# A two-layer graph attention kernel: where layer 2's one-hot matrices lie, when they are loaded, and when layer 2's gathers may begin

## The chip, the cores and the metric

The kernel runs on one core of a Trainium2 chip. Its time is the device time of one execution in microseconds. Beside the times there is one profiled execution, taken by the hardware profiler; its trace lists every instruction with its start, its length and what ended the wait before it. The engines are TensorE (PE; its weight loads are listed as PEld), VectorE (DVE), ScalarE (ACT), GpSimd (POOL) and SyncE (SP). SP, ACT and POOL also issue DMA transfers, which all run on the core's 16 DMA engines.

## The reference

A layer norm and a relu are applied to 3125 nodes of 768 features. Then come two graph attention layers over 53,125 edges (each edge in both directions, and a loop for every node), sorted by their target node:

```
xl = (x @ W).reshape(n, heads, out_ch)
e = leaky_relu(alpha_src[src] + alpha_dst[dst], 0.2)
alpha = softmax of e over the edges of one target
out = segment_sum(xl[src] * alpha, dst) + bias
```

Layer 1 has 4 heads of 256 columns, followed by a layer norm, a relu and a residual product `h0 @ Wr1 + br1`. Layer 2 has one head of 768 columns, followed by a layer norm and `h1 @ Wr2 + br2`. The input is added at the end.

## The kernel before

The nodes are cut into 25 blocks of 128 targets (the last has 53). Every block owns J = 17 lists of 128 edge slots, its tiles; the last block uses 8 of them. The work of a layer has three parts.

**The products.** `x @ W` gives a table in HBM, one row for each node, and two numbers for each node, alpha_src and alpha_dst. In layer 1's sums the function `end1` (L1217) finishes a block: it normalizes, turns the block with PE, multiplies by W2 (L1260), and stores a block of `h1T_d` and a block of `table2` through SP's queue. Layer 2 can gather when all of table2 is stored.

**The weights of the edges.** For each edge the kernel needs alpha_src of its source and alpha_dst of its target. Both are picked by products with one-hot matrices. These were made in layer 1 and kept in HBM, in fp8, as `hot_d`: for each block 128 rows of 2176 + 640 + 425 bytes. In layer 2 a loop over the 25 blocks (L1355) multiplies them: 51 matmuls of 25 columns (`source_values`, L552) and 5 of 24 columns (`own_products`, L535) for each block. DVE then masks and sums the results (L554, L541, L557). I call this the one-hot loop. The matrices lie in a ring of 4 buffers (`load_hot`, L1288). The first four blocks are loaded through POOL's queue (L1292), the others through SP's, each when the loop has come to it and a buffer is free (L1357). After the loop, `shares` (L644) turns the sums into weights, with two scans on DVE.

**The sums.** `sums` (L704) goes over the blocks and in each over five rounds of tiles. `fetch` (L769) gathers 128 rows of the table for each tile with one indirect DMA on POOL (L779), and PE adds them, weighted, into the block's rows (L826). In layer 1 the gathers go to 13 buffers of 4096 bytes, g0 to g12 in turn; there are 416 of them. In layer 2 they go to a ring of 26 buffers of 771 words (`ahead` is 26), also 416 of them. Between the rounds PE does other work that the code hands out in steps. In layer 2 that is the residual product `h1 @ Wr2` (L1326, and L1330 for the bias), 18 matmuls for each block, one block ahead. The residual of block 0 is done near the end of the one-hot loop (`fill`, L1367).

**The order.** PE's order is written out by hand in the one-hot loop, and PE's, ACT's and DVE's in the sums. Everything else is ordered by a planner that goes by its own estimates; every queue runs its instructions in order. Two rules bear on the change. `behind` is a copy of one number on POOL (L1370, into `mark`), which waits for the sums of one block of the one-hot loop; all gathers of layer 2 stand behind it on POOL's queue. `last_hot` is the last load of a one-hot matrix; what SP loads for the sums stands behind it on SP's queue.

Layer 2's tiles lie in the memory that layer 1 leaves, and a tile waits only for those that lay in its own place. The layer-2 constants, wr2, the four one-hot buffers and three buffers of h1 end at one point; the 26 gather buffers begin there, each taking 3104 bytes.

Of the kernel before, what the change touches and what calls it, by code (L numbers as in the profile page):

```python
# [10 lines left out]
F32 = mybir.dt.float32  # L11
F32R = mybir.dt.float32r
BF16 = mybir.dt.bfloat16
F8 = mybir.dt.float8e4
# [9 lines left out]
PE = mybir.EngineType.PE  # L24
# [16 lines left out]
HOT = 3264  # L41
# [28 lines left out]
def in_order(  # L70
# [16 lines left out]
    nc = tc.nc  # L87
# [6 lines left out]
    NB = -(-N // P)  # L94
# [22 lines left out]
    def rows_of(b):  # L117
        return P if b < NB - 1 else LAST
# [4 lines left out]
    def tiles_of(b):  # L123
        return J if b < NB - 1 else JL
# [64 lines left out]
    def load_rows(q, t, src_, b):  # L189

        for o, e in pieces(b):
            q.dma_start(t[o:e], src_[b * P + o:b * P + e, :])
# [306 lines left out]
    def parts_of(pool, v, n, name):  # L499

        part = pool.tile([P, 3, n], BF16, name=name, bufs=1)
        rest = pool.tile([P, n], F32, name=name + "_r", bufs=1)
        nc.vector.tensor_copy(part[:, 0, :], v)  # L503
        nc.vector.tensor_sub(rest, v, part[:, 0, :])
        nc.vector.tensor_copy(part[:, 1, :], rest)
        nc.vector.tensor_sub(part[:, 2, :], rest, part[:, 1, :])
        return part
# [15 lines left out]
    def by_quarter(t, v, n, heads):  # L523

        for i in range(3):
            nc.vector.tensor_tensor(t[:, :, :, i, :], v(i)[:, :, None, :].to_broadcast([P, n, 4, 2 * heads]),
                                    mine[:, None, :, None].to_broadcast([P, n, 4, 2 * heads]), OP.mult)

    def own_products(heads, pp, oh, tabd_b, bufs=1):

        n = 6 * heads
        pd = pp.tile([128, 512], F32, name="pd", bufs=bufs)[:, :J * n]
        for c in range(WIN // 128):
            o = FROM[c % 4] + c // 4
            nc.tensor.matmul(pd[:, o * n:(o + 4) * n], oh[:, c * 128:(c + 1) * 128],  # L535
                             tabd_b.rearrange("p q t v -> p (q t v)"), start=(c == 0), stop=True,
                             skip_group_check=True)
        return pd.rearrange("p (j t v) -> p v j t", t=3, v=2 * heads)

    def own_values(own, b, pd):  # L540
        nc.vector.tensor_reduce(own[:, :, :, b].rearrange("p j v -> p v j"), pd, axis=AX.X, op=OP.add)  # L541
# [162 lines left out]
    def sums(heads, cols, table, al, alo_d, ahead, lag, gp, ap, pp, end, more, pace, first=None, delay=0.0):  # L704
# [4 lines left out]
        width = heads * cols  # L709
        f = width // 2  # L710
# [48 lines left out]
        def ask(b):  # L759
            ao = asked[b] = ap.tile([128, 2 * heads, NB], F32, name="ao", bufs=3)  # L760
            nc.gpsimd.indirect_dma_start(
                out=ao.rearrange("p v b -> p (v b)"), out_offset=None, in_=alo_d[:, :],
                in_offset=bass.IndirectOffsetOnAxis(ap=at_last[:, b:b + 1], axis=0))

        extra = 3 if heads == 1 else 0
        turns = count()
        owns = {}

        def fetch(b, k):  # L769

            got = {}
            for j in ROUNDS[k]:
                if j >= tiles_of(b):
                    continue
                if heads == 1:
                    g = gp.tile([128, width + extra], F32, name="g", bufs=ahead)
                else:
                    g = gp.tile([128, width], F32, name=f"g{next(turns) % ahead}", bufs=1)
                nc.gpsimd.indirect_dma_start(  # L779
                    out=g[:, :width], out_offset=None, in_=table[:, :],  # L780
                    in_offset=bass.IndirectOffsetOnAxis(ap=idx_s[:, b * J + j:b * J + j + 1], axis=0))
                if heads == 1:
                    nc.scalar.activation(g[:, width:], alo_d[:, POS[j], b, :], AF.Copy)
                got[j] = g, weights_of(b, j)
                place = PLACE[j]
                if place == 4:
                    own = owns[b] = ap.tile([128, width], F32, name="own", bufs=3)
                    load_rows(nc.sync, own, table, b)
                if heads > 1 and b == 1 and place == 11:
                    ask(0)  # L790
                if heads > 1 and b and place == (13 if tiles_of(b) == J else 5):
                    ask(b)
            return got

        def weights_of(b, j):

            c = b * J + j
            lo, hi = 32 * QUARTERS[j][0], 32 * QUARTERS[j][-1] + 32
            w = ap.tile([128, heads, hi - lo], F32, name=f"w{hi - lo}", bufs=9 if hi - lo == 32 else 3)
            if heads == 1:  # L800
                nc.vector.tensor_scalar(w[:, 0, :], iota_f[:, lo:hi], rel_s[:, c:c + 1], al[:, POS[j], 0, b:b + 1],  # L801
                                        op0=OP.is_equal, op1=OP.mult)
            else:
                oh = ap.tile([128, 68], F32, name="oh", bufs=4)[:, :hi - lo]
                nc.vector.tensor_scalar(oh, iota_f[:, lo:hi], rel_s[:, c:c + 1], None, op0=OP.is_equal)  # L805
                nc.vector.tensor_tensor(w, oh[:, None, :].to_broadcast([128, heads, hi - lo]),  # L806
                                        al[:, POS[j], :, b:b + 1].to_broadcast([128, heads, hi - lo]), OP.mult)
            return w
# [33 lines left out]
    with tc.tile_pool(name="m1", bufs=1) as mp:  # L842
# [8 lines left out]
        with tc.tile_pool(name="h0", bufs=1) as hp, tc.tile_pool(name="pm1", bufs=1, space=PSUM) as pm1, \  # L851
# [5 lines left out]
            so = right.enter_context(tc.tile_pool(name="so1", bufs=1, side="right"))  # L857
# [415 lines left out]
    with tc.tile_pool(name="m2", bufs=1, reuse_waits="tile") as mp, \  # L1273
# [12 lines left out]
        hots = {}  # L1286

        def load_hot(b, q):  # L1288
            hots[b] = mp.tile([128, HOT], F8, name="hot", bufs=4)
            return q.dma_start(hots[b][:, :S + WIN + J * NB], hot_d[b, :, :S + WIN + J * NB]).ins  # L1290

        for b in range(4):  # L1292
# [8 lines left out]
        def load_h1(b, q):  # L1301
            h1 = h1s[b] = mp.tile([128, NK2, P], F32, name="h1", bufs=3)
            r = rows_of(b)
            q.dma_start(h1[:, :, :r], h1T_d[b][:, :, :r])

        for b in range(2):
            load_h1(b, nc.gpsimd)
        loaded = {}

        def load(b):  # L1310
# [26 lines left out]
        def ahead_of(first, end, apart):  # L1337
            load(first)
            load(first + 1)
            for b in range(first, end):  # L1340
                load(b + 2)
                yield from residual(b, apart)

        with tc.tile_pool(name="ps2", bufs=1, space=PSUM, reuse_waits="tile") as pp:
            fill = ahead_of(0, FIRST, 5)
            with tc.tile_pool(name="so2", bufs=1, side="right", reuse_waits="tile") as so, \
                    tc.manual_schedule(engines={PE}):
                al = wide[:, :, None, :]
                with tc.tile_pool(name="sb2", bufs=2, side="right", reuse_waits="tile") as sb:
                    part = parts_of(sb, asad2.rearrange("p b v -> p (b v)"), NB * 2, "part")  # L1350
                    v = lambda i: part[:, i, :].rearrange("p (b v) -> p b v", v=2)
                    by_quarter(tabd, v, NB, 1)
                    for i in range(3):
                        nc.vector.tensor_copy(tabs[:, i], v(i)[:, :, :1].rearrange("p b h -> p h b"))
                    for b in range(NB):  # L1355
                        if b not in hots:
                            last_hot = load_hot(b, nc.sync)  # L1357
                        hot = hots.pop(b)
                        pick = picks.pop() if picks else mp.tile([128, J, 1, NB], F32, name="pick", bufs=2)
                        source_values(1, al, b, pp, 3, J, hot, tabs,  # L1360
                                      hot[:, S + WIN:S + WIN + J * NB].rearrange("p (j b) -> p j b", b=NB), pick)
                        own_values(own, b, own_products(1, pp, hot[:, S:S + WIN], tabd[:, b]))
                        if b == NB - 10:
                            with tc.issue_after(last_hot):
                                load(0)
                        if b > NB - 4:
                            with tc.issue_after(last_hot):  # L1367
                                next(fill)
                        if b == NB - 11:
                            behind = nc.gpsimd.tensor_copy(mark, al[:, 0, 0, b:b + 1]).ins  # L1370
                with tc.tile_pool(name="sr2", bufs=1, side="right", reuse_waits="tile") as sr:
                    shares(wide, own, al2[:, :, 0, :], ends2, sr, pp, fill, (5, 4))
                for _ in fill:
                    pass
# [493 lines left out]
```

## Time and profile before

| | |
|---|---|
| three runs | 1989.29 us (median), 1982.86 to 1989.85 |
| the profiled execution | 1990.46 us, of which 1988.6 are the span of the trace |
| PE busy | 1793.4 us, 90% |
| DVE busy | 1060.1 us, 53% |
| POOL busy | 902.0 us, 45% |
| HBM traffic | 290 GB/s over the span |
| last layer-1 gather issued | 1210.57 us |
| last store of table2 issued | 1268.28 us |
| first matmul of the one-hot loop | 1270.99 us |
| first matmul of layer 2's sums | 1368.75 us |

Busy time is an average over stages with different limits. A group's row gives the line, the engine, the operation, its tiles and its count, then busy time and the mean of one instruction in ns, then how long its engine sat idle just before it and what ended that. "issue" is time in which an engine waited for nothing that the profile shows. In a row of a timeline the first number is the start in us, the second the length, and the bracket the idle time before it with what ended it. A row of windows has a stretch and its length, then busy time and count for PE, PEld, DVE, ACT and POOL, then the granted TensorE clock, the mean busy share of the 16 DMA engines, and what they moved.

### The profile page before, as it was taken

What the parts mean: (1) busy time and instruction counts of PE and PEld (TensorE: products, weight loads), DVE (VectorE), ACT (ScalarE), POOL (GpSimd) and SP (SyncE); (2) the same over time, 40 slices, a digit from 0 to 9 for tenths busy, and PEclk for the clock granted to TensorE, in tenths of its full rate; (3) what the DMA queues carried; (4) which work ended last, traced back from release to release, by engine and by line L of the source; (5) the groups of instructions that cost most, each with busy time, mean ns of one, the idle gap of its engine ahead of it and who ended that gap; (6) DMA issues with size and microseconds to landing.
All of it is one profiled execution on the core that took longest, in us unless ns stands there. A gap on an engine that the chain in (4) does not pass through costs nothing. (4 is left out here: it accounts for less than half of the span.)

```text
span 1988.6 us, 34126 instructions
## 1 busy us (share of the span) xinstructions
PE 1793.4 (90%) x12558; PEld 985.9 (50%) x12558; DVE 1060.1 (53%) x3030; ACT 295.5 (15%) x1094; POOL 902.0 (45%) x977
## 2 busy tenths in 40 slices
PE   8999999998779999999998998838989888998986
PEld 5666665664446555565544554534333333333332
DVE  7673437886645555655566454524444444444445
ACT  2122331001211221221111211101000000000000
POOL 2000101112455566566656653052666666666662
PEclk9999999998889999999999999858999998999999
DMA  7823448774699999999999996486999999999984
GB/s 244 267 96 132 129 144 205 177 176 152 229 408 352 386 375 396 381 381 408 391 392 367 376 362 264 142 286 207 338 327 327 328 328 325 330 338 323 341 284 147
DMA packets 180786, 574.86 MB, mean 289 GB/s; under 512 B 32768, under 2 KB 55034, under 8 KB 180485
## 3 DMA queue, kind: packets, MB, share of 16 engines
q0 software_dynamic: 108432, 408.63, 57.5%
q1 hardware_dynamic: 67786, 153.57, 22.5%
q10 hardware_dynamic: 4394, 10.39, 1.3%
q8 instruction: 103, 1.69, 0.3%
q14 instruction: 71, 0.57, 0.1%
HBM read 503.27 MB, written 73.85 MB: 290 GB/s over the span
## 5 line engine op out<-in xcount | busy, mean ns | idle before, releaser
L779 POOL DMA_INDIRECT g<-table,idx_s x832 | 816.3, 981 | 555.6 <-issue 208.6
L826 PE MATMUL pa<-g,w 128*32 128x256 f32 (+2 forms) x5868 | 527.9, 429 | 69.5 <-issue 52.6
L826 PEld LDWEIGHTS pa<-g,w 128*32 128x32 f32 x5868 | 204.5, 111 | 360.8 <-issue 238.2
L1326 PE MATMUL pr<-wr,h 128*128 128x384 f32 (+1 forms) x800 | 299.2, 509 | 26.7 <-issue 26.3
L1260 PE MATMUL p<-w,h1T 128*128 128x384 f32 (+2 forms) x800 | 280.3, 497 | 5.2 <-DVE h1T L1246 2.6
L801 DVE TENSOR_SCALAR w<-iota_f,rel_s,al 128x32 f32<-128x32 f32 (+1 forms) x416 | 102.3, 318 | 264.1 <-PE pa L826 156.1
L1326 PEld LDWEIGHTS pr<-wr,h 128*128 128x128 f32 (+1 forms) x800 | 143.7, 190 | 182.1 <-issue 112.6
L1260 PEld LDWEIGHTS p<-w,h1T 128*128 128x128 f32 (+1 forms) x800 | 143.9, 187 | 127.8 <-issue 34.1
L806 DVE TENSOR_TENSOR w<-oh,al 128x128 f32<-128x128 f32 (+1 forms) x416 | 131.8, 317 | 124.8 <-PE pa L826 54.0
L931 PE MATMUL pm<-w,h0l 128*128 128x344 f32 (+1 forms) x468 | 144.2, 463 | 0.0
L1191 PE MATMUL pr<-h0k,wr 128*128 128x256 f32 (+1 forms) x576 | 141.8, 392 | 2.4 <-issue 2.2
L1068 PE MATMUL pm<-h0g,wr 128*128 128x512 f32 x288 | 134.2, 614 | 0.0
L931 PE MATMUL pm<-w,h0g 128*128 128x344 f32 x432 | 130.0, 456 | 0.3 <-ACT h0g L910 0.3
L1191 PEld LDWEIGHTS pr<-h0k,wr 128*128 128x128 f32 x576 | 106.3, 190 | 33.4 <-issue 13.0
L999 POOL DMA_DIRECT2D hot_d<-ohd x25 | 13.5, 540 | 222.7 <-DVE own L503 126.6
L805 DVE TENSOR_SCALAR oh<-iota_f,rel_s 128x32 f32<-128x32 f32 (+1 forms) x416 | 110.4, 265 | 0.5 <-issue 0.2
L492 ACT ACTIVATE bn_sd<-bn_mv,eps 128x1 f32<-128x1 f32 (+1 forms) x50 | 14.7, 294 | 638.6 <-DVE bn_mv L488 445.3
L931 PEld LDWEIGHTS pm<-w,h0l 128*128 128x128 f32 (+1 forms) x468 | 86.6, 189 | 45.7 <-issue 8.4
L931 PEld LDWEIGHTS pm<-w,h0g 128*128 128x128 f32 x432 | 81.4, 192 | 40.3 <-issue 0.9
L1068 PEld LDWEIGHTS pm<-h0g,wr 128*128 128x128 f32 x288 | 54.4, 197 | 58.0 <-issue 57.9
L552 PE MATMUL pq<-tabs,hot 128*128 128x25 bf16 x1275 | 41.7, 180 | 39.4 <-issue 35.5
L1244 ACT ACTIVATE h1T<-p,be_c,g_c 128x128 f32<-128x128 f32 (+1 forms) x200 | 72.0, 476 | 18.3 <-PE p L1239 12.6
(306 smaller groups left out, 1439.5 us busy)
## 6 DMA issues: line engine op xcount, KB each, us to landing
s<-slo_d SPq DMA_DIRECT2D x25, 544.0 KB
g<-table,idx_s POOLq DMA_INDIRECT x832
table<-row SPq DMA_DIRECT2D x24, 512.0 KB
own<-table SPq DMA_DIRECT2D x24, 512.0 KB
h1T_d<-h1T SPq DMA_DIRECT2D x24, 512.0 KB
h<-h1T_d SPq DMA_DIRECT2D x22, 512.0 KB
ring<-in_x_dram SPq DMA_DIRECT2D x24, 384.0 KB
table<-row SPq DMA_DIRECT2D x24, 384.0 KB
```

The source lines that it names most:

```text
L552: nc.tensor.matmul(q[:, j], oh[:P, o:o + 128], tabs[:, i], start=(i == 0), stop=(i == 2))
L779: nc.gpsimd.indirect_dma_start(out=g[:, :width], out_offset=None, in_=table[:, :], in_offset=bass.IndirectOffsetOnAxis(ap=idx_s[:, b * J + ...
L801: nc.vector.tensor_scalar(w[:, 0, :], iota_f[:, lo:hi], rel_s[:, c:c + 1], al[:, POS[j], 0, b:b + 1], op0=OP.is_equal, op1=OP.mult)
L805: nc.vector.tensor_scalar(oh, iota_f[:, lo:hi], rel_s[:, c:c + 1], None, op0=OP.is_equal)
L806: nc.vector.tensor_tensor(w, oh[:, None, :].to_broadcast([128, heads, hi - lo]), al[:, POS[j], :, b:b + 1].to_broadcast([128, heads, hi - ...
L826: nc.tensor.matmul(pa[32 * q:32 * q + 32, o // f, o % f:o % f + m], w[:, o // cols, :], g[:, o:o + m], start=to not in opened, stop=False, ...
L931: nc.tensor.matmul(pm[:r, :C], h0[b][:, k, :], w1[:, k, i * C:(i + 1) * C], start=(k == 0), stop=(k == NK1 - 1))
L1068: nc.tensor.matmul(pm, wr1[:, k, m * 128:(m + 1) * 128], groups[gi][:, k, :], start=(k == 0), stop=(k == NK1 - 1))
L1191: nc.tensor.matmul(pm[:, :n], wr1[:, k, m * 128:(m + 1) * 128], loaded[i, k][:, :n], start=(k == 0), stop=(k == NK1 - 1))
L1244: nc.scalar.activation(hT[:, k0 + k, :r], pt[:, k, :r], AF.Relu, bias=be1_c[:, k0 + k:k0 + k + 1], scale=g1_c[:, k0 + k:k0 + k + 1])
L1260: nc.tensor.matmul(pm[:, :n], hT[:, k, :r], w2[:, k, o:o + n], start=(k == 0), stop=(k == NK2 - 1))
L1326: nc.tensor.matmul(pm[:, :384], h1[:, k, :r], wr2[:, k, i * 384:(i + 1) * 384], start=(k == 0), stop=False)
```

## The change

Every one-hot matrix from block 4 on gets a place of its own: 21 places of 3264 bytes in a pool that begins where the gather buffers will begin, behind a pad of 27520 bytes. Block b takes place (b + 3) mod 21, so that blocks 18 to 24 have the first seven places and blocks 4 to 17 the other fourteen. The matrices of blocks 4 to 17 are loaded through POOL's queue, ahead of the two loads of h1 that were on that queue already; those of 18 to 24 through SP's queue. None of the loads stands in the loop any more.

The gather buffers, which are made when the pool of the matrices has been closed, get fixed places, `g0` to `g25`, and are used in the order 0 to 7, 17 to 25, 8 to 16 (`TURNS`). A gather waits for the matrices that lay in its place.

`behind` is made after block 1 of the loop in place of block 14 (NB - 11).

```diff
         extra = 3 if heads == 1 else 0
         turns = count()
+        if heads == 1:
+            TURNS = [*range(8), *range(17, ahead), *range(8, 17)]
+            spare = {s: gp.tile([128, width + extra], F32, name=f"g{s}", bufs=1) for s in range(ahead)}
...
                 if heads == 1:
-                    g = gp.tile([128, width + extra], F32, name="g", bufs=ahead)
+                    s = TURNS[next(turns) % ahead]
+                    g = spare.pop(s, None) or gp.tile([128, width + extra], F32, name=f"g{s}", bufs=1)
...
         def load_hot(b, q):
-            hots[b] = mp.tile([128, HOT], F8, name="hot", bufs=4)
+            if b < 4:
+                hots[b] = mp.tile([128, HOT], F8, name="hot", bufs=4)
             return q.dma_start(hots[b][:, :S + WIN + J * NB], hot_d[b, :, :S + WIN + J * NB]).ins
...
-        for b in range(2):
-            load_h1(b, nc.gpsimd)
         loaded = {}
...
-            with tc.tile_pool(name="so2", bufs=1, side="right", reuse_waits="tile") as so, \
-                    tc.manual_schedule(engines={PE}):
+            with tc.manual_schedule(engines={PE}):
                 al = wide[:, :, None, :]
-                with tc.tile_pool(name="sb2", bufs=2, side="right", reuse_waits="tile") as sb:
+                with tc.tile_pool(name="hb", bufs=1, reuse_waits="tile") as hb, tc.tile_pool(name="sb2", bufs=2, side="right", reuse_waits="tile") as sb:
                     part = parts_of(sb, asad2.rearrange("p b v -> p (b v)"), NB * 2, "part")
+                    hb.tile([128, 27520], F8, name="pad")
+                    places = [hb.tile([128, HOT], F8, name=f"hot{i}") for i in range(NB - 4)]
+                    for b in range(4, NB):
+                        hots[b] = places[(b + 3) % (NB - 4)]
+                    for b in range(4, 18):
+                        load_hot(b, nc.gpsimd)
+                    for b in range(18, NB):
+                        last_hot = load_hot(b, nc.sync)
+                    for b in range(2):
+                        load_h1(b, nc.gpsimd)
...
                     for b in range(NB):
-                        if b not in hots:
-                            last_hot = load_hot(b, nc.sync)
                         hot = hots.pop(b)
...
-                        if b == NB - 11:
+                        if b == 1:
                             behind = nc.gpsimd.tensor_copy(mark, al[:, 0, 0, b:b + 1]).ins
```

The pool `so2`, which held nothing, is gone.

## The prediction

> **What bounds the kernel now.** I read the page first: 1988.6 us of span, 1990.46 us for that execution, against a median of 1989.29 (1982.86 to 1989.85). The sum below is made against 1990.46; the median lies 1.2 us (0.06%) under it, so it needs no correction. The page's slices show where PE is not near its limit: 26 and 27 of 40, each 49.7 us, so about 1243 to 1342 us.
>
> ```profile
> PE   8999999998779999999998998838989888998986
> DMA  7823448774699999999999996486999999999984
> ```
>
> That is the turn from layer 1 to layer 2. I cut it by the work: the one-hot loop (L1355) runs from its first matmul at 1270.96 to its last residual matmul at 1356.63. The windows view of its three stretches (columns: length, PE, PEld, DVE, ACT, POOL busy with counts, clock, DMA share, GB/s):
>
> ```profile
> 1270.96:1299.96 29.00, 24.48 (x891) 23.92 (x891) 19.98 (x48) 0.00 (x0) 0.18 (x1) 0.62 0.71 221
> 1299.96:1337.60 37.64, 6.81 (x111) 4.94 (x112) 2.14 (x6) 0.00 (x0) 24.71 (x26) 0.50 0.86 305
> 1337.60:1356.63 19.03, 16.48 (x417) 13.48 (x415) 10.41 (x25) 0.00 (x0) 0.00 (x0) 0.71 0.86 302
> ```
>
> A block is 51 + 5 matmuls (L552, L535) and one pick on DVE (L554); counting the picks, the stretches hold 16, 2 and 7 blocks. So a block costs 29.00/16 = 1.81 us, then 19 us, then normal again. What ends PE's waits, by groups of the loop, and the rows of PE's timeline:
>
> ```profile
> L552 PE MATMUL pq<-tabs,hot 128*128 128x25 bf16 x1275 | 41.7, 180 | 39.4 <-issue 35.5 <-DVE tabs L1354 3.3 <-DMA hot<-hot_d 0.7
> L1326 PE MATMUL pr<-wr,h 128*128 128x384 f32 x12 | 6.0, 632 | 0.0
> ```
> ```profile
> 1270.99 1.53 PE L552 MATMUL pq<-tabs,hot 128*128 128x25 bf16 x51 [3.26 <-DVE tabs L1354]
> 1272.37 0.29 PE L535 MATMUL pd<-tabd,hot 128*128 128x24 bf16 x5
> 1272.50 1.52 PE L552 MATMUL pq<-tabs,hot 128*128 128x25 bf16 x51
> ...
> 1278.56 0.76 PE L552 MATMUL pq<-tabs,hot 128*128 128x25 bf16 x24 [0.76 <-issue]
> 1279.18 0.27 PE L535 MATMUL pd<-tabd,hot 128*128 128x24 bf16 x5
> 1279.31 1.46 PE L552 MATMUL pq<-tabs,hot 128*128 128x25 bf16 x51
> 1280.61 0.29 PE L535 MATMUL pd<-tabd,hot 128*128 128x24 bf16 x5
> 1280.74 1.30 PE L552 MATMUL pq<-tabs,hot 128*128 128x25 bf16 x43
> 1282.58 0.39 PE L552 MATMUL pq<-tabs,hot 128*128 128x25 bf16 x8 [0.54 <-issue]
> ...
> 1304.77 0.30 PE L552 MATMUL pq<-tabs,hot 128*128 128x25 bf16 x5 [0.46 <-issue]
> 1306.23 0.28 PE L552 MATMUL pq<-tabs,hot 128*128 128x25 bf16 x4 [1.16 <-issue]
> ...
> 1323.33 0.18 PE L552 MATMUL pq<-tabs,hot 128*128 128x25 bf16 x1 [1.91 <-issue]
> 1325.43 0.18 PE L552 MATMUL pq<-tabs,hot 128*128 128x25 bf16 x1 [1.92 <-issue]
> ```
>
> Not data but "issue": PE waits for its own instructions. Between the two small gaps lie 24+5+51+5+43 = 128 matmuls, 256 instructions with their weight loads: code comes in pieces of that size. Later every single matmul waits 1 to 2 us. That begins and ends with POOL's gathers (POOL's timeline), and DVE starves too, waiting for nothing that is named (DVE's):
>
> ```profile
> 1299.21 0.18 POOL L1370 COPY mark<-wide 128x1 f32<-128x1 f32 x1 [39.68 <-DVE wide L557]
> 1300.50 1.02 POOL L779 DMA_INDIRECT g<-table,idx_s  x1 [1.11 <-DMA hot<-hot_d]
> ...
> 1331.88 0.95 POOL L779 DMA_INDIRECT g<-table,idx_s  x1 [0.30 <-issue]
> 1371.78 0.94 POOL L779 DMA_INDIRECT g<-table,idx_s  x1 [38.95 <-PE pa L826]
> ```
> ```profile
> 1274.74 0.58 DVE L557 TENSOR_REDUCE wide<-pick 128x17 f32<-128x425 f32 x1
> ...
> 1298.56 0.59 DVE L557 TENSOR_REDUCE wide<-pick 128x17 f32<-128x425 f32 x1
> ...
> 1312.74 0.60 DVE L554 TENSOR_TENSOR pick<-pq,hot 128x425 f32<-128x425 f32 x1 [11.04 <-remote]
> ```
>
> The copy to mark releases 26 gathers, one per 1.25 us (0.95 + 0.30), all the ring holds; while they move, code hardly arrives. Undisturbed, the loop would be 25 x 1.81 + 6.0 (the 12 residual matmuls) = 51.3 us; it takes 85.67. **The excess is 34.4 us, 1.32 us for each of the 26 gathers.**
>
> After the loop PE is the bound again: the longest POOL wait above ends on "PE pa", the ring being full, and the first matmul of the sums and a window of the main loop read
>
> ```profile
> 1368.75 3.90 PE L826 MATMUL pa<-g,w 128*32 128x384 f32 x16 [4.00 <-issue]
> ```
> ```profile
> 1500.00:1600.00 100.00, 89.80 (x461) 35.82 (x460) 44.33 (x134) 8.16 (x72) 66.84 (x69) 0.98 0.92 332
> ```
>
> PE is busy 90%. All 26 gathers have landed before its first matmul at 1368.75, so what the one-hot loop wins moves the end one for one.
>
> **The change, part by part.** (1) *Own places.* Twenty-one matrices get places of 3264 bytes behind a pad of 27520; SP's 21 loads no longer wait for a free buffer. Those waits lay beside PE's work: in the first stretch PE misses hot data for under 1 us (the 0.7 above). Third stretch: 7 x 1.81 + 6.0 = 18.7 against 19.03. Worth 0.3 us; I count 0.
>
> (2) *14 loads through POOL.* They follow the eight wr2 loads on POOL's queue:
>
> ```profile
> 1219.17 0.54 POOL L1298 DMA_DIRECT2D wr<-in_L_gnn_Wr_dram  x1 [0.48 <-DMA hot<-hot_d]
> 1220.21 0.54 POOL L1298 DMA_DIRECT2D wr<-in_L_gnn_Wr_dram  x1 [0.51 <-DMA hot<-hot_d]
> 1258.47 1.06 POOL L1304 DMA_DIRECT2D h<-h1T_d  x2 [37.72 <-DVE h1T L1246]
> ```
> ```profile
> hot<-hot_d POOLq DMA_DIRECT2D x4, 405.1 KB
> ```
> ```profile
> 1225.00:1250.00 25.00, 23.29 (x98) 12.31 (x93) 14.21 (x40) 4.68 (x13) 0.00 (x0) 1.00 0.24 98
> 1250.00:1275.00 25.00, 20.38 (x205) 11.06 (x205) 7.59 (x27) 4.63 (x13) 1.06 (x2) 0.90 0.27 83
> ```
>
> At that pace (1.04 us each) they issue from 1221 to 1236. Their places lie over layer 1's gather buffers g0 to g11, and layer 1's 416 gathers are 32 full turns of 13, so the last turn frees them in that order; the last is freed by
>
> ```profile
> 1236.47 1.92 PE L826 MATMUL pa<-g,w 128*32 128x256 f32 x16
> ```
>
> so by 1240 all are issued. Behind them on POOL stand only the two h1 loads, which wait until 1258 anyway. 14 x 405 KB is 5.7 MB; the DMA is 76% idle for 50 us. Cost: 0 if PE's code keeps coming. At the dear end, code came slowly there under gathers too:
>
> ```profile
> 1202.42 1.63 PE L826 MATMUL pa<-g,w 128*32 128x256 f32 x18
> ...
> 1209.22 1.48 PE L826 MATMUL pa<-g,w 128*32 128x256 f32 x9 [0.18 <-issue]
> 1210.63 4.80 PE L1260 MATMUL p<-w,h1T 128*128 128x384 f32 x12
> 1215.36 1.93 PE L826 MATMUL pa<-g,w 128*32 128x256 f32 x32
> ```
>
> 32 matmuls took 8.2 us (1202.42 to 1210.63) in place of 1.9: 6.3 us for a piece of code that is late. Between 1221 and 1268 PE runs some 180 matmuls, so one or two pieces begin: 0 to 12.6 us. I take 0: the row at 1215.36 shows 32 matmuls at full pace while the first four hot loads and the wr2 loads, the same kind, are in flight.
>
> (3) *Mark after block 1, not 14.* Block 1's sums end at 1275.32 (1274.74 + 0.58); as the gather at 1300.50 follows sums that ended at 1299.15, the first goes out about 1276.7. The added waits: slots 0 to 7 lie under the pad and are free. The ninth gather uses slot 17, which begins 17 x 3104 = 52,768 bytes in, 25,248 past the pad, so over places 7 and 8, matrices 4 and 5; it waits for block 5; the next eight wait for one block more each, to 13. The last nine (slots 8 to 16) wait for 18 to 24. Behind a waiting gather POOL has only gathers, and PE needs the first at L826 after the loop. So gathers come in doses:
>
> - First eight: 10 us of issue (8 x 1.25), to 1286.7, moving until about 1289 (an estimate: one or two are under way behind the last issue). PE has code until about 1281.5: the piece due at 1277.80 was asked for before them, and 128 matmuls last 3.5 us (1278.56 to 1282.04). Lost, 1281.5 to 1289: **8 us**, bounds 0 and 10.6 (8 x 1.32).
> - Nine behind blocks 5 to 13, and six behind 18 to 23 (three go out at or past the loop's end). Each moves for 1.25 us and no more come until PE has finished a block. Bounds per gather: 0, when it falls between two fetches; 1.32, the rate of the 26. A fetch is under way for half of a piece's time or more, and 1.32 was measured with the queue never empty, so I take 0.8: **12 us**, bounds 0 and 20.
>
> (4) *Seven loads through SP* from layer 1's end, 2.8 MB in the first 10 us at the worst, beside the first eight gathers: included in the 8.
>
> Sum: 51.3 + 8 + 12 = 71.3 against 85.67, **14.4 us less: 1976**.
>
> The Trainium skill, "Runtime: NRT & Kernel Launch", Instruction fetch mechanics, says that code comes in blocks of 256 instructions, the next one fetched while the current runs, and that crossing is mostly hidden. The trace agrees on the 256 and not on "hidden" (0.5 to 1 us, then 35 us); by the rule the loop would be rival 1's. The Trainium skill's "DMA: Bandwidth & Descriptors", Queues, rings and completion order, says that a DMA engine turns between its queues a packet at a time. By that a piece would wait for one gather's share, 1.25 us: eleven pieces, 14 us, 65 in all and a time of 1970. The trickle of one matmul per 2 us shows many turns for one piece, so I keep 0.8 for each gather.
>
> **Rivals.** *1. Doses do not hurt.* Code slips between spaced gathers; the loop takes 51.3, or 25 x 1.51 + 6.0 = 43.8 without any gap (a block from 1270.99 to 1272.50). Gain 34 to 42: 1948 to 1956. For: in the first stretch, at 0.71 DMA share, gaps stayed under 1 us. Against: those loads were no gathers.
> *2. The cost only moves.* Every gather costs its 1.32 us wherever it falls in the loop: 23 x 1.32 = 30.4, loop 81.7, and the SP loads beside it: gain 0 to 4, 1986 to 1991.
> *3. Slower: layer 1's end pays.* The 14 POOL loads starve PE's code there, 12.6 us by (2), while the loop gains as rival 2 or less: 1999 to 2003. It decides once the loss before 1268 is more than the loop's gain, so two late pieces outweigh rival 2 and not the forecast. For: PE is 93% busy in 1225 to 1250, without reserve. Against: the row at 1215.36.
> *4. It does not do what it says*: a place is still held until 1258 (h1T), the 14 loads and the mark queue behind it, and gathers start near 1300 as now: 1990.
>
> **How the numbers follow.** Forecast 0.48 (own spread 1966 to 1984, of which 0.13 lies above 1980), rival 1 0.14, rival 2 0.20, rival 3 0.15, rival 4 0.03. The range leaves out rival 3 and the cheap half of rival 1: 1955 to 1995. Half a percent (10 us, about what a measurement can tell from no change): faster 0.35 + 0.14 = 0.49; same 0.13 + 0.17 + 0.03 = 0.33; slower 0.15 + 0.03 (rival 2 with SP's loads dearer) = 0.18.
>
> **What would show it.** Right: first layer-2 gather near 1277; hot loads on POOL between 1221 and 1240 with no new "issue" gaps there; a slow patch of PE at 1281 to 1289, then blocks of 2 to 3 us; loop end near 1342; main loop of the same length. Wrong: blocks of 4 us or more through the middle (rival 2), "issue" gaps before 1268 (rival 3), or a longer main loop, which would mean that the gathers' start decided more than the loop.

## The result and the profile after

The changed kernel takes 1969.28 us (median of 6 runs, 1965.16 to 1975.85) against 1989.17 us of the kernel before, timed beside it (6 runs, 1982.86 to 1990.34). The ratio is 0.9912, 95% interval 0.9893 to 0.993. The forecast was 1976 and 1955 to 1995. The profiled execution took 1969.17 us with a span of 1967.3.

The page's slices of PE first (40 slices, now of 49.2 us each; busy share in tenths):

```profile
PE   8999999998779999999999999869988898898896
```

The hole in PE at slice 27, a 3 before, is a 6. The rest of the row is what it was within a digit. The sums, from their first matmul to the end of the span, hold no gain (windows view; length, then busy time and count of PE, PEld, DVE, ACT, POOL, then clock, DMA share, GB/s). Before:

```profile
1368.75:1988.60 619.85, 543.30 (x2772) 219.72 (x2772) 276.78 (x839) 51.53 (x442) 386.81 (x390) 0.96 0.87 307
```

After:

```profile
1347.63:1967.30 619.67, 540.83 (x2772) 215.77 (x2772) 276.02 (x839) 51.86 (x442) 384.27 (x390) 0.95 0.87 307
```

619.85 and 619.67: the sums have only moved. PE idles in them too, for 619.67 - 540.83 = 78.8 us after the change. Of these, 65.4 us are "issue": 34.5 before the residual products (row of the page, all of it in the sums) and 30.9 before L830 (waits view of the sums).

```profile
L1329 PE MATMUL pr<-wr,h 128*128 128x384 f32 (+1 forms) x800 | 304.6, 512 | 36.9 <-issue 34.5
```

390 gathers go out in that time. It is the same kind of wait as in the one-hot loop, in a place that the change does not touch; no run here spaces those gathers, so whether they are its cause there is open.

What lies between the loop and them has the same length too (1347.63 - 1335.37 = 12.26 after, 1368.75 - 1356.48 = 12.27 before). The loop itself, first one-hot matmul to first matmul of the shares (L674), has gone from 85.49 to 66.91 us. These 18.6 us are the gain of 21.3 us in the span, but for 2.5 us by which layer 1 ended earlier (the loop begins at 1268.46, before at 1270.99). I take these 2.5 us for chance: in the profiles below the loop begins anywhere between 1265.1 (e6) and 1281.5 (e3). The group of the loop's matmuls and that of the gathers, after:

```profile
L552 PE MATMUL pq<-tabs,hot 128*128 128x25 bf16 x1275 | 42.6, 181 | 19.4 <-issue 16.1 <-DVE tabs L1366 3.3
L783 POOL DMA_INDIRECT g<-table,idx_s x26 | 26.8, 1030 | 40.0 <-DVE wide L557 24.7 <-PE pq L552 7.5 <-issue 6.9
```

PE's wait for "issue" is down from 35.5 to 16.1, 19.4 less. The gathers now wait for the loop's blocks (24.7 and 7.5) where they came in one row. POOL's timeline:

```profile
1217.57 0.54 POOL L1295 DMA_DIRECT2D hot<-hot_d  x1 [0.68 <-DMA wr<-in_L_gnn_Wr_dram]
...
1234.52 0.54 POOL L1295 DMA_DIRECT2D hot<-hot_d  x1 [2.41 <-PE pa L830]
1254.35 1.06 POOL L1309 DMA_DIRECT2D h<-h1T_d  x2 [19.29 <-DVE h1T L1250]
1272.77 0.18 POOL L1380 COPY mark<-wide 128x1 f32<-128x1 f32 x1 [17.35 <-DVE wide L557]
1273.74 1.02 POOL L783 DMA_INDIRECT g<-table,idx_s  x1 [0.79 <-DMA hot<-hot_d]
...
1282.61 0.95 POOL L783 DMA_INDIRECT g<-table,idx_s  x1 [0.30 <-issue]
1291.10 0.94 POOL L783 DMA_INDIRECT g<-table,idx_s  x1 [7.54 <-PE pq L552]
1292.43 0.94 POOL L783 DMA_INDIRECT g<-table,idx_s  x1 [0.39 <-DVE wide L557]
...
1309.15 0.95 POOL L783 DMA_INDIRECT g<-table,idx_s  x1 [2.10 <-DVE wide L557]
1318.89 0.94 POOL L783 DMA_INDIRECT g<-table,idx_s  x1 [8.79 <-DVE wide L557]
...
1336.94 2.74 POOL L783 DMA_INDIRECT g<-table,idx_s  x1 [0.30 <-issue]
```

Fourteen loads between 1217 and 1235, eight gathers in a row, nine behind blocks 5 to 13, nine behind 18 to 24, the last two of these after the loop's end at 1335.37. And PE's timeline:

```profile
1274.30 0.48 PE L552 MATMUL pq<-tabs,hot 128*128 128x25 bf16 x13
1275.09 0.26 PE L552 MATMUL pq<-tabs,hot 128*128 128x25 bf16 x4 [0.31 <-issue]
...
1285.25 0.26 PE L552 MATMUL pq<-tabs,hot 128*128 128x25 bf16 x3 [1.15 <-issue]
1285.35 0.29 PE L535 MATMUL pd<-tabd,hot 128*128 128x24 bf16 x5
1285.48 1.51 PE L552 MATMUL pq<-tabs,hot 128*128 128x25 bf16 x51
1289.40 0.29 PE L535 MATMUL pd<-tabd,hot 128*128 128x24 bf16 x5 [2.40 <-DVE own L541]
...
1291.02 1.17 PE L552 MATMUL pq<-tabs,hot 128*128 128x25 bf16 x38
1292.38 0.26 PE L552 MATMUL pq<-tabs,hot 128*128 128x25 bf16 x3 [0.19 <-issue]
...
1295.64 1.06 PE L552 MATMUL pq<-tabs,hot 128*128 128x25 bf16 x34
```

Beside the first eight gathers one block takes 11.18 us (1274.30 to 1285.48), one to four matmuls at a time; beside the spaced ones two blocks take 4.62 (1291.02 to 1295.64). There is also a wait that was not forecast, "DVE own", 2.40 us. DVE's timeline names its cause:

```profile
1288.34 0.33 DVE L663 TENSOR_SCALAR pen<-pen 100x641 bf16<-100x641 bf16 x1 [9.43 <-DMA pen<-near_d]
```

`pen` is a tile of the shares. Its operation stands in DVE's queue in the middle of the loop's, its data was late, and all later sums of the loop stood behind it. SP's queue, before and after:

```profile
1269.63 1.29 SPq L661 DMA_DIRECT2D pen<-near_d  x4
```
```profile
1266.92 3.50 SPq L1295 DMA_DIRECT2D hot<-hot_d  x7
1270.51 1.81 SPq L192 DMA_DIRECT2D xr<-in_x_dram  x3
1273.14 4.03 SPq L661 DMA_DIRECT2D pen<-near_d  x4
```

Once the loads no longer wait inside the loop, seven of them and three of xr go ahead of pen. Before, L663 ran at 1273.75 and waited for nothing.

### The profile page after: what moved, and what is told of

Read it like the earlier page. It is cut to its first block, busy times and chain, and to the rows that moved or that the text cites. A ratio compares the mean times of both kernels' runs of the same rounds, so it can differ in the third digit from the quotient of the medians.

```text
span 1967.3 us, 34126 instructions
## 1 busy us (share of the span) xinstructions
PE 1794.7 (91%) x12558; PEld 986.9 (50%) x12558; DVE 1058.8 (54%) x3030; ACT 296.9 (15%) x1094; POOL 910.2 (46%) x991
## 5 line engine op out<-in xcount | busy, mean ns | idle before, releaser
L830 PE MATMUL pa<-g,w 128*32 128x256 f32 (+2 forms) x5868 | 520.3, 433 | 61.2 <-issue 46.7
L830 PEld LDWEIGHTS pa<-g,w 128*32 128x32 f32 x5868 | 202.8, 111 | 344.5 <-issue 227.4
L1329 PE MATMUL pr<-wr,h 128*128 128x384 f32 (+1 forms) x800 | 304.6, 512 | 36.9 <-issue 34.5
L1264 PE MATMUL p<-w,h1T 128*128 128x384 f32 (+2 forms) x800 | 285.6, 504 | 4.9 <-DVE h1T L1250 2.6
L1195 PEld LDWEIGHTS pr<-h0k,wr 128*128 128x128 f32 x576 | 106.3, 190 | 30.5 <-issue 10.6
L1003 POOL DMA_DIRECT2D hot_d<-ohd x25 | 13.5, 539 | 218.8 <-DVE own L503 122.7
L554 DVE TENSOR_TENSOR scr<-pq,ohh 128x500 f32<-128x500 f32 x100 | 56.8, 596 | 29.1 <-PE pq L552 22.8
```

What stands on the lines that cost most here:

```text
L554: nc.vector.tensor_tensor(pick[:, j0:j0 + n], q, ohh[:, j0:j0 + n, None, :].to_broadcast([128, n, heads, NB]), OP.mult)
L830: nc.tensor.matmul(pa[32 * q:32 * q + 32, o // f, o % f:o % f + m], w[:, o // cols, :], g[:, o:o + m], start=to not in opened, stop=False, ...
L1195: nc.tensor.matmul(pm[:, :n], wr1[:, k, m * 128:(m + 1) * 128], loaded[i, k][:, :n], start=(k == 0), stop=(k == NK1 - 1))
L1264: nc.tensor.matmul(pm[:, :n], hT[:, k, :r], w2[:, k, o:o + n], start=(k == 0), stop=(k == NK2 - 1))
L1329: nc.tensor.matmul(pm[:, :384], h1[:, k, :r], wr2[:, k, i * 384:(i + 1) * 384], start=(k == 0), stop=False)
```

## The experiments

**The theory:** PE starves while gathers move in an unbroken row; the gain comes from breaking the row, whatever breaks it. **The rivals:** (A) the places and the early loads are the gain; (B) the early start is the gain; (C) what is left of the loss in the changed kernel comes from the late load of pen (the masks for the scans) or from SP's seven loads, and not from its first eight gathers. Every row below comes from a profiled execution: the loop, PE's "issue" wait in the group of L552, and the time from the sums' first matmul to the end. Median and ratio are those of the timed runs; the ratio is against the kernel before as timed beside them (median 1987.76 for e1 to e4, 1985.65 for e5 to e8, 1988.99 for e9 to e12), so that ratios and not medians compare across these sets.

| kernel | loop | issue | sums | median | ratio (95%) |
|---|---|---|---|---|---|
| before | 85.5 | 35.5 | 619.9 | 1989.17 | |
| after | 66.9 | 16.1 | 619.7 | 1969.28 | 0.9912 (0.9893 to 0.993) |
| e1: before, mark after block 1 | 86.8 | 34.8 | 620.1 | 1989.7 | 1.001 (0.9997 to 1.0022) |
| e2: before, mark after block 24 | 54.2 | 8.4 | 642.1 | 1980.54 | 0.9959 (0.9942 to 0.9976) |
| e3: after, mark after block 14 | 76.0 | 19.7 | 617.8 | 1978.07 | 0.9957 (0.9934 to 0.998) |
| e4: after, mark after block 24 | 53.4 | 6.0 | 641.5 | 1977.8 | 0.994 (0.9918 to 0.9961) |
| e5: before, gathers spaced | 64.3 | 7.3 | 619.2 | 1967.28 | 0.9908 (0.9891 to 0.9924) |
| e6: after, first eight spaced | 69.3 | 13.0 | 616.6 | 1968.46 | 0.9926 (0.9906 to 0.9946) |
| e7: after, all loads on SP | 68.5 | 17.2 | 619.9 | 1970.81 | 0.993 (0.9911 to 0.9949) |
| e8: after, turns in order | 61.3 | 11.2 | 621.4 | 1963.76 | 0.9886 (0.987 to 0.9903) |
| e9: after, pen first | 75.6 | 13.1 | 619.9 | 1976.83 | 0.9942 (0.9919 to 0.9965) |
| e10: pen first, turns in order | 68.9 | 10.6 | 621.4 | 1973.14 | 0.9934 (0.991 to 0.9958) |
| e11: before, spaced later | 60.4 | 10.5 | 624.9 | 1968.26 | 0.99 (0.9877 to 0.9923) |
| e12: after again | 68.3 | 15.9 | 620.5 | 1971.18 | 0.9907 (0.988 to 0.9935) |

### e1 to e4: the mark alone

e1, in the kernel before:

```diff
-                        if b == NB - 11:
+                        if b == 1:
```

> The kernel before with the mark after block 1, nothing else: one ring of 4 one-hot buffers, gather buffers that lie elsewhere, so all 26 gathers go out in one row from about 1276. Theory (gathers in flight starve PE of code, and what the change wins it wins because the places dose the gathers): the starved stretch only moves to the front of the loop, its excess stays 30 to 36 us, 1984 to 1994. Rival A (the loads taken out of the loop win the time): no gain either, 1989. Rival B (the early start of the gathers wins it): like the changed kernel, 1966 to 1974.

The 26 gathers go out in one row from 1274.64 to 1306.99, and PE's "issue" wait is what it was:

```profile
L552 PE MATMUL pq<-tabs,hot 128*128 128x25 bf16 x1275 | 41.6, 181 | 39.8 <-issue 34.8 <-DVE tabs L1354 3.3 <-DMA hot<-hot_d 1.8
```

The early start alone is worth nothing. Rival B falls.

e2, in the kernel before, and e4, in the changed kernel:

```diff
-                        if b == NB - 11:
+                        if b == NB - 1:
```
```diff
-                        if b == 1:
+                        if b == NB - 1:
```

> The kernel before with the mark after block 24, nothing else: no gather moves while the loop runs. Theory: no starved stretch, the loop falls from 85.7 to about 51 us and the first matmul of the sums comes about 34 us earlier; the sums then start with few gathers landed and may give back up to 15 us: 1955 to 1972. Rival A: the loads through the ring are the cost, the loop stays long and the gathers come late: 1990 to 2010. Rival B: gathers that start later make it slower by the delay, about 2005.

> The changed kernel with the mark after block 24: loads early and no gather beside the loop. Theory: the loop at 44 to 51 us, the sums' first matmul 15 us earlier than in the changed kernel, up to 15 us given back by gathers that come late: 1952 to 1972. Rival A: 1966 to 1972 at best. Rival B: slower than the kernel before.

The loop came out near what was expected (about 51, and 44 to 51), at 54.2 and 53.4 us: this is the loop without gathers, now measured. The times did not. The row of gathers lay beside the shares and the first sums, and there PE starved in the same way; PE's timeline of e4:

```profile
1336.09 4.08 PE L830 MATMUL pa<-g,w 128*32 128x384 f32 x16 [4.22 <-issue]
...
1350.23 0.69 PE L1329 MATMUL pr<-wr,h 128*128 128x384 f32 x1 [2.35 <-issue]
1353.03 0.80 PE L1329 MATMUL pr<-wr,h 128*128 128x384 f32 x1 [2.11 <-issue]
...
1367.72 2.80 PE L830 MATMUL pa<-g,w 128*32 128x384 f32 x12 [1.30 <-issue]
```

Single matmuls every 2.1 to 2.8 us, other lines and other data than in the loop, the same starving. The sums grew by 22 us (642.1 and 641.5 against 619.9 and 619.7), more than the "up to 15" on record. The row does not stop at 26 there: in e2 thirty gathers go out 1.25 us apart, from 1329.21 to 1367.38, because PE's sums free buffers while it runs, and 21 of them stand after the sums' first matmul (1340.39). What was expected of the sums was wrong; that a row of gathers costs PE about 1 us for each wherever it falls (22/21) is what the two runs add.

e3, in the changed kernel:

```diff
-                        if b == 1:
+                        if b == NB - 11:
```

> The changed kernel with the mark back after block 14: own places and early loads stay, but 17 gathers may go in one row. Theory: about 17 x 1.3 = 22 us lost in that row in place of some 15 to 16 in the changed kernel, so 1974 to 1982. Rival A: as the changed kernel, 1966 to 1972. Rival B: as before, 1985 to 1992.

With the mark at its old block the 17 gathers whose places are already free go in one row (1314.10 to 1335.18), the last nine wait for their places; the loop takes 76.0. (The profiled execution was 11 us over its median, but its loop also began some 10 us later than most, at 1281.5.) 1978.07 is as expected. About half of the loop's gain is there without the early mark (9.5 of 18.6 us); in this layout the early mark brings the other half, as it lets blocks 5 to 13 break the row as well.

### e5 and e11: the old layout, spaced

In the kernel before, a copy to mark after every block from 1 on, and the k-th gather, counted from 0, behind block k + 1 (the last two behind block 24 as well):

```diff
+                with tc.issue_after(dose[min(next(issued), len(dose) - 1)]) if dose else ExitStack():
+                    nc.gpsimd.indirect_dma_start(
...
-                        if b == NB - 11:
-                            behind = nc.gpsimd.tensor_copy(mark, al[:, 0, 0, b:b + 1]).ins
+                        if b > 0:
+                            behinds.append(nc.gpsimd.tensor_copy(mark, al[:, 0, 0, b:b + 1]).ins)
...
```

> The kernel before with one mark after every block from 1 on, and the k-th gather behind the mark of block k + 1: old ring of 4 one-hot buffers, loads through SP, gather buffers as before; only the gathers are spaced, one for each block. Theory (bursts of gathers starve PE of code; what the change wins is the spacing): loop at 58 to 66 us, 1962 to 1974 in all. Rival A (own places and loads out of the loop win it): 1984 to 1992. Rival B (an early start wins it): between, some 1975, since the last gathers go out at the loop's end.

Loads in a ring of 4, in the loop, through SP, as before; only the row is broken. POOL's timeline and PE's group:

```profile
1284.92 0.97 POOL L781 DMA_INDIRECT g<-table,idx_s  x1 [0.48 <-issue]
1286.16 0.18 POOL L1373 COPY mark<-wide 128x1 f32<-128x1 f32 x1 [0.27 <-issue]
1286.82 0.97 POOL L781 DMA_INDIRECT g<-table,idx_s  x1 [0.48 <-issue]
```
```profile
L552 PE MATMUL pq<-tabs,hot 128*128 128x25 bf16 x1275 | 40.0, 181 | 18.1 <-DMA hot<-hot_d 7.3 <-issue 7.3 <-DVE tabs L1357 3.3
```

One gather per block, and "issue" falls from 35.5 to 7.3, less than e2 has without any gather in the loop (8.4). What is left is 7.3 us of waiting for one-hot matrices, which e2, with the same loads and no gathers beside them, does not have. The loop is still 10.1 us longer than e2's. 1967.28 is the whole gain without the new places, so rival A falls. It also says what the new places do in the changed kernel: the gathers of later turns wait for them, and that wait is the spacing.

e11 is e5 with block `min(k + 11, 24)` in place of k + 1, so that half of the gathers fall together at the loop's end:

> The old layout (kernel before) with the spaced gathers of e5, but the k-th is let go behind block min(k + 11, 24) and not behind block k + 1, so that some 13 gathers run spaced beside the loop's second half and the other 13 fall together at its end. Theory: a spaced gather costs the loop 0.4 to 0.6 us (5 to 8 us for 13, loop 57 to 61), and the late ones lie beside the 12 us of the shares and the first sums, where e2 lost 22 us with 26 together; half of them lose 2 to 8 us there (sums 621 to 627). Time 1961 to 1969. Rival: what counts at the loop's end is that gathers come together at all, not how many; then the sums grow by over 10 us (630 or more) and the time is 1970 to 1978.

Loop 60.4, sums 624.9: 3.9 us won in the loop, 5.7 given back in the sums, 1968.26. The theory's sizes held, and there is nothing to win in that direction.

### e6 to e8: what is left in the changed kernel

e6 was to space the first eight gathers: DVE writes their indices anew after blocks 1 to 8.

```diff
+                        if 1 <= b <= 8:
+                            j = [j for r in ROUNDS for j in r][b - 1]
+                            nc.vector.scalar_tensor_tensor(first_idx[b - 1], al[:, 0, 0, b:b + 1], 0.0, idx_s[:, j:j + 1],
+                                                           op0=OP.mult, op1=OP.add)
...
```

> The changed kernel, with the first eight gathers spaced too: their row numbers are written again by VectorE (number plus 0 times a sum of block 1, 2, ... 8), so that the k-th of them waits for block k; eight small VectorE instructions more. Theory: the starved patch at blocks 4 to 5, about 12 us in the changed kernel, shrinks to some 4: 1957 to 1965. Rival C (that patch comes from the late load of the masks for the scans, or from SP's seven loads, and not from the gathers): 1966 to 1972.

"issue" fell by 3 us only, from 16.1 to 13.0, and a wait of 6.18 took its place, in PE's timeline of e6:

```profile
1282.94 0.29 PE L535 MATMUL pd<-tabd,hot 128*128 128x24 bf16 x5 [6.18 <-DVE own L541]
```

It is the wait for pen again, as DVE's timeline has it (the trace names a gather as what ended the wait, but L663 reads nothing but pen):

```profile
1281.88 0.33 DVE L663 TENSOR_SCALAR pen<-pen 100x641 bf16<-100x641 bf16 x1 [8.31 <-DMA g<-table,ix]
```

DVE also writes the indices, so the gathers behind this wait came late and then together. POOL's timeline has seven of them 1.25 us apart, and PE starves beside them as beside the old row:

```profile
1291.38 0.94 POOL L783 DMA_INDIRECT g<-table,ix  x1 [1.88 <-issue]
...
1298.88 0.95 POOL L783 DMA_INDIRECT g<-table,idx_s  x1 [0.30 <-issue]
```
```profile
1297.09 0.27 PE L552 MATMUL pq<-tabs,hot 128*128 128x25 bf16 x4 [1.17 <-issue]
```

The block in which this row stands takes 8.9 us (1293.53 to 1302.40) where an undisturbed one takes 1.5. So the edit moved the row more than it broke it, and it is no test of eight spaced gathers. The expected 1957 to 1965 was missed; 1968.46 lies where rival C put it, and pen's late load is part of the reason. That the gathers have no part in it does not follow: the starving went where the row went.

e7 sends the fourteen loads through SP:

```diff
-                        load_hot(b, nc.gpsimd)
+                        load_hot(b, nc.sync)
```

> The changed kernel with all 21 one-hot loads on SP's queue after layer 1, none through POOL at its end: 5.7 MB more to move beside the first gathers, and no load beside layer 1's last products. Theory: blocks 4 to 17 wait for their matrices or their code a little longer, 3 to 10 us lost: 1971 to 1980. Were layer 1's end paying for the POOL loads (the slower rival of the prediction), it would be faster: under 1966. If where the loads stand does not matter: 1967 to 1971.

1970.81 lies on the border of the two answers on record, and within what e12 shows of the changed kernel itself: which queue the fourteen loads take makes no difference that these runs can tell. It is not the only thing that moved, though: in e7 pen's operation stands at the loop's end on DVE (L663 at 1334.00) and waits for nothing, so PE is free of that wait, and more loads move beside the loop. Two effects may cancel here.

e8 uses the gather buffers in the order 0 to 25, so that the ninth gather waits for block 18:

```diff
-            TURNS = [*range(8), *range(17, ahead), *range(8, 17)]
+            TURNS = [*range(ahead)]
```

> The changed kernel with the buffers used in the order 0 to 25: the ninth gather then waits for block 18, no gather goes out beside blocks 5 to 17, and 18 are left for the loop's end and the time behind it. Theory: blocks 6 to 18 run undisturbed and win 4 to 6 us, the row of gathers behind block 20 starves the loop's end and the start of the sums and costs 8 to 16: 1971 to 1982. Rival B (early gathers win): slower still, above 1985. If spacing does not matter: 1967 to 1971.

This was missed on the good side: 1963.76, the lowest median of all, ratio 0.9886 (0.987 to 0.9903; the intervals of the changed kernel's two sets, 0.9893 to 0.993 and 0.988 to 0.9935, overlap with it). POOL's timeline:

```profile
1283.46 0.95 POOL L783 DMA_INDIRECT g<-table,idx_s  x1 [0.30 <-issue]
1314.18 0.94 POOL L783 DMA_INDIRECT g<-table,idx_s  x1 [29.77 <-DVE wide L557]
...
1336.50 0.95 POOL L783 DMA_INDIRECT g<-table,idx_s  x1 [0.30 <-issue]
```

Nothing is gathered beside blocks 5 to 17, and eleven late gathers fall behind the loop's end (1330.55), nine of them into the 12 us of the shares, where PE has 20 residual matmuls (1331.14 to 1337.76) and then idles for some 4 us in every kernel here. Loop 61.3 and sums 621.4, against 66.9 and 619.7 (68.3 and 620.5 in e12). e4, which puts all 26 there, shows where that hiding ends.

### e9, e10 and e12: pen first

e9 issues the four loads of pen on SP ahead of the one-hot loads, from a tile in the pool of the layer-2 constants; e10 is e9 with the turns of e8; e12 is the changed kernel again.

```diff
+        pen = mp.tile([4 * NB, WIN + 1], BF16, name="pen")
+        for q in range(4):
+            nc.sync.dma_start(pen[q * NB:(q + 1) * NB], bass.AP(
...
```

> The changed kernel with the four loads of pen issued on SP right after ball_r, ahead of the one-hot loads; all else as it is. Theory: in the changed kernel DVE's L663 waited 9.43 us for pen, PE 2.40 us behind it, because seven one-hot and three xr loads go ahead of pen on SP. With pen first, L663 waits for nothing, the first patch shrinks by 2 to 3 us, the loop takes 64 to 65 us and the time is 1965 to 1968. Rival: the wait for pen lies inside the time in which PE is starved of its instructions anyway; then L663's wait goes, PE's gaps in blocks 4 to 7 stay, the loop takes 66 to 69 us and the time is that of the changed kernel, 1967 to 1971.

> The kernel of e9 with the gathers' turns 0 to 25 in order (the turns of e8). Theory: the two gains add, as they lie in different stretches of the loop: e8's loop of 61.25 us less 2 to 3 us of the wait for pen, that is 58 to 59.5 us, and a time of 1959 to 1963. Rival: pen's wait hides in the starved patch; then it is e8 again, loop 60 to 63 us, 1963 to 1966.

> The changed kernel itself, unaltered, beside the three others on one chip. By its runs so far 1967 to 1971, with a loop of 66 to 69 us and the sums at 619 to 621. If its loop differs by over 2 us between two profiles, differences of that size in the loops of e6, e7 and e9 tell nothing by themselves.

e12 is as on record. Both others came out slower than on record, 1976.83 and 1973.14, and the trace says that they tried something else. POOL's timeline, DVE's and PE's, of e10:

```profile
1206.87 0.60 POOL L1295 DMA_DIRECT2D hot<-hot_d  x1
1244.19 1.64 POOL L1295 DMA_DIRECT2D hot<-hot_d  x3 [36.72 <-DVE z L1228]
...
1268.15 0.54 POOL L1295 DMA_DIRECT2D hot<-hot_d  x1 [0.50 <-DMA hot<-hot_d]
```
```profile
1278.45 0.33 DVE L659 TENSOR_SCALAR pen<-pen 100x641 bf16<-100x641 bf16 x1 [11.45 <-DMA pen<-near_d]
```
```profile
1279.51 0.29 PE L535 MATMUL pd<-tabd,hot 128*128 128x24 bf16 x5 [9.60 <-DVE own L541]
```

The extra tile moves everything that is placed behind it, and the second one-hot load now waits 36.72 us for a tile that layer 1 still uses. The fourteen loads behind it on POOL go out until just past the loop's start (1266.98), and pen, first on SP at 1265.32, is there only 13 us later; that those loads hold it up is inferred from the times. PE's wait for pen's operation is 9.60 us where e8 has 3.46. So these two show the price of a place that is held too long, some 8 us of loop (68.9 against 61.3 in e10 and e8; e9's 75.6 against the 66.9 and 68.3 of the changed kernel points the same way, though its profiled execution was 13 us over its median and its loop began as late as 1280.7). It is a part of the prediction's rival 4, a place still held and loads queued behind it, brought about by an edit. Whether pen's wait can be had back is left open; e7 has none, and its loop is no shorter. e12's loop of 68.3 against 66.9 says that differences of 1.5 us between single profiles mean nothing.

## Why the prediction was right, step by step

**The loop without gathers, 51.3.** Right within 3 us: e2 and e4 measure 54.2 and 53.4. Within e4's 53.4 lies a wait of 3.09 us for pen (its row is below), which the forecast did not have; it is 50.3 without it.

**Why the loop was long: gathers in an unbroken row, 1.32 us each.** Shown: e1 moves the row and the loss goes with it, e2 takes it out of the loop, e5 breaks it. By e2's loop it is (85.5 - 54.2)/26 = 1.20, and (86.8 - 54.2)/26 = 1.25 in e1. That PE waits for its own instructions while they move is still an inference. For it speaks a row of the page that is the same in every kernel here (packets, MB, share):

```profile
q8 instruction: 103, 1.69, 0.3%
```

PE has 12,558 matmuls and as many weight loads, 25,116 instructions, 98 pieces of 256: about as many packets as this queue moved, if it is PE's. No run took PE's instructions out of the way, so why gathers hold them up was not tried.

**Own places, 0.** Right as far as the runs tell: e5 has the gain without them. In the changed kernel the 7.3 us of waits for one-hot data that e5 has are gone, and the wait for pen and the starving beside the first eight gathers, which e5 lets go one by one, stand in their place.

**Fourteen loads through POOL, 0 (bounds 0 and 12.6).** Right. They went out from 1217.57 to 1234.52 (on record: 1221 to 1240), and in that stretch the DMA engines were full and PE too (window of the changed kernel):

```profile
1217.00:1237.00 20.00, 20.00 (x104) 10.28 (x101) 9.33 (x26) 3.71 (x10) 7.51 (x14) 1.00 1.02 405
```

Rival 3 fell with it: from 1217.57 to the loop's first matmul at 1268.46 PE's timeline has no wait for "issue". 104 matmuls are less than one piece of 128, so the row is a weak test of how code fares beside such loads.

**First eight gathers, 8 us.** Size right, place and cause partly wrong. The changed kernel with its gathers in the loop and out of it, e4, differ in block 4 by 11.18 - 3.69 (1276.06 to 1279.75 in e4) = 7.5 us, and in block 5, with pen's wait, by 4.05 - 4.73 = -0.7: 6.8 us. PE's timeline of e4 for these two blocks:

```profile
1276.06 0.83 PE L552 MATMUL pq<-tabs,hot 128*128 128x25 bf16 x27
1278.95 0.81 PE L552 MATMUL pq<-tabs,hot 128*128 128x25 bf16 x24 [2.06 <-issue]
1279.61 0.29 PE L535 MATMUL pd<-tabd,hot 128*128 128x24 bf16 x5
1279.75 1.51 PE L552 MATMUL pq<-tabs,hot 128*128 128x25 bf16 x51
1284.35 0.29 PE L535 MATMUL pd<-tabd,hot 128*128 128x24 bf16 x5 [3.09 <-DVE own L541]
```

So the wait for pen is there without any gather. The slow patch lay at 1275 to 1285, not at 1281 to 1289. The step that failed is "PE has code until about 1281.5", which rested on "the piece due at 1277.80 was asked for before them": PE began to starve at 1274.8, 13 matmuls into block 4 and 1 us after the first gather. In e1, whose gathers began at the same point of the loop, it starves from 27 matmuls into block 4, where e4 has its gap too, so being the next piece did not protect it. Why the changed kernel starves 14 matmuls sooner than that is not shown. That the loss came out near 8 us although the patch began 6 us early and ended 4 us early is partly luck. Pen's wait was in no step: the seven loads on SP were counted for the DMA beside the first gathers, and not for what now stands behind them on SP's own queue.

**The spaced gathers, 0.8 each.** This term was mis-sized. 66.9 - 53.4 - 6.8 leaves 6.7 us for the 16 that fell in the loop, 0.42 each, where 15 at 0.8 gave 12. It is a remainder of single profiles, good to about 0.1 each (1.5 us over 16, by e12). e5 gives the same size by another way: its loop is 10.1 us longer than e2's with 23 gathers in it, 0.44 each, though there it shows as waits for one-hot data and not as "issue". The 0.8 was chosen between two bounds with the argument that a fetch is under way for half of a piece's time or more; no run shows how long a fetch is under way. With these terms the loop is 66.9 (by the way the 6.7 is worked out) where the forecast had 71.3. These 4.4 us and the 2.5 us of layer 1's earlier end, which no step forecast, are what the profiled execution lies below 1976.

**What would show it.** First gather 1273.74 (on record near 1277), loop end 1335.37 (near 1342), blocks of 2.3 us beside spaced gathers (2 to 3), no "issue" wait beside the fourteen loads, sums of the same length: as written, but for the place of the slow patch.

**The two rules.** The Trainium skill, "Runtime: NRT & Kernel Launch", Instruction fetch mechanics, has the crossing from one block of instructions to the next mostly hidden. In e4 and e2, without gathers, "issue" waits of 6.0 and 8.4 us of a loop of 54 were not hidden, and with the row 35.5. The Trainium skill's "DMA: Bandwidth & Descriptors", Queues, rings and completion order, has a DMA engine turn between its queues a packet at a time. The prediction's estimate by that rule was 14 us of loss and a time of 1970; 13.5 us and 1969.28 were measured. This total was the better one, but the way to it was not: the one piece or so beside the eight gathers took some 10 us, not one gather's 1.25, and the spaced ones cost less than 1.25.

Rival 1 (doses do not hurt) fell by 13.5 us of loop, rival 2 (the cost only moves) holds for a row, by e1, and fell for spaced gathers, by e5.

## What to carry to other kernels

If an engine waits for "issue" and not for data while many indirect gathers are in flight, do not ask first where they should start, but whether they can be let go one at a time, each behind a step of the work beside them; a copy of one number per step was enough here. Moving the same row earlier won nothing, and moving it later gave 22 us of the loop's 31 back in the sums. A load that no longer waits in a loop goes ahead of whatever stands behind it on its queue, so look for the small tile there that an in-order engine needs soon.

## What the runs showed of the hardware

- Beside indirect gathers 1.25 us apart PE loses 1.0 to 1.25 us for each, in the one-hot loop (bf16, 128 by 25; e1, e2) and in the sums (f32, 128 by 384; e2, e4) alike; at one for each block of some 2 us it loses 0.42 (changed kernel) or 0.44 (e5 against e2).
- Plain loads did not do this in the one stretch that shows it: at a share of 1.02 of the DMA engines and 405 GB/s PE was busy 20.00 of 20.00 us, while the row of gathers starved it at 0.86 and 305 GB/s. With 104 matmuls in the stretch that is a weak test.
- A new tile of 1282 bytes in front of others went with 5.7 us more (e9 against e12, whose intervals overlap) and 9.4 us more (e10 against e8, timed in another set), with a load that waited 36.72 us for its place.
